# Field-pair products on one core: the order of a store's 128 rows inside its block of the output

## The chip, the cores and the metric

The kernel runs on one core of a Trainium2 chip. The metric is the device time of one execution in microseconds (us), less is better. Before the change it is 1285.48 us, the median of three runs.

## What is computed

The input is `x` with 4096 records of 32 fields of 64 numbers, and a 64 x 64 matrix `W`. Every field is multiplied by `W`, and for each of the 496 pairs of fields i < j the untouched field i is multiplied, number by number, with the transformed field j:

```python
vid = jnp.einsum('bfd,de->bfe', x, W)
idx_i, idx_j = jnp.triu_indices(32, k=1)
return x[:, idx_i, :] * vid[:, idx_j, :]        # 4096 x 496 x 64, float32
```

The output is 4096 x 496 x 64 x 4 bytes, 520 MB, against 33.6 MB of input. The order in which the kernel leaves the output in DRAM is its own choice: the host puts the numbers into the reference's order afterwards, and the time does not hold that step.

## The kernel before, in words

**Layout.** The 128 partitions of the on-chip memory are 2 halves of the batch times 64 numbers of a field. A "unit" is 128 records, 512 bytes in a partition. The 4096 records make 16 tiles of 2 x 128 records; a tile is 32 units of `x`, one for each field. The one large buffer `mem` (line 183) has 445 units in each partition, for the loaded `x` and the finished products together. PSUM holds `vid`, the 32 transformed fields of one tile.

**Work.** For each tile (loop at line 276) TensorE makes `vid` in two halves of 16 fields (lines 321 to 335), and VectorE forms the 496 products of the tile, one `tensor_tensor` for each run of pairs with one pattern (line 304). Over 16 tiles that is 7936 units of output in each partition. They are cut into 74 pieces, the `SLOTS` (line 28): each entry has the count n of units (48 to 128), the place in `mem` where they are put, and some seams at which a product is cut. 26 of the 74 slots have 128 units.

**Stores.** When the last product of a slot is made, `store` (line 261) sends it out as one DMA: 128 partitions with n units each. A partition's n units lie side by side in `mem` and in DRAM, so each partition is one row of n x 512 bytes, up to 65,536. The blocks of the slots lie one behind the other in the output (`BLOCKS`, line 62). Line 265 lays the rows in a block: row p, that is partition p, lies at place p of the block. After each of the two load groups one store is cut into a leading part of `LEAD` = 28 units and the rest (lines 267 to 270), so there are 76 stores.

**Order.** SP's queue (the issuing engine SyncE) carries the loads and the stores of slots 0 to 45, ScalarE's (ACT) those of slots 46 to 73 (`SECOND`, line 43). The input comes in two groups: tile 0 in two transfers and tiles 1 to 7 in three, at the start (lines 221 to 257); tiles 8 to 15 in three more in the middle (line 278). A store waits for VectorE's products (the semaphore `made`), and VectorE waits, before it writes units of `mem`, until the store that reads them has landed (`after`, line 204). The program sets these waits from the units that the transfers touch; the transfer and the waits are issued in `transfer` (line 197, the DMA itself line 199). There are 8 loads and 76 stores, 84 DMAs.

Of the kernel before, what the change touches and what calls it, by code (L numbers as in the profile page):

```python
# [10 lines left out]
P = 128  # L11

C = 128
# [30 lines left out]


LEAD = 28


PAD = 24
# [6 lines left out]
def row(n):  # L56

    return n
# [3 lines left out]
BLOCKS = [0, *accumulate(P * row(n) for n, *_ in SLOTS)]  # L62
# [112 lines left out]
def pairwise_bilinear_kernel(nc, x0, x, out):  # L175
# [8 lines left out]
    mem = ctx.enter_context(nc.sbuf_tensor([P, UNITS, C], F32))  # L184
# [3 lines left out]
    made = nc.alloc_semaphore("made")  # L188
# [8 lines left out]
    def transfer(out_, in_, units, reads, needs, queue=sp):  # L197
        sem = nc.alloc_semaphore(f"moved{len(moved)}")
        queue.issue(lambda: queue.engine.dma_start(out=out_, in_=in_), needs).then_inc(sem, 16)
        queue.note(sem, 16)  # L200
        moved.append((units, reads, sem))
        return sem
# [58 lines left out]
    def store(slot, last):  # L261
        nonlocal hold
        begin, end = STARTS[slot : slot + 2]
        home = SLOTS[slot][1]
        rows = out[BLOCKS[slot] : BLOCKS[slot + 1], :].rearrange("(p u) c -> p u c", p=P)
        parts = [(0, end - begin, (made, last), act if slot >= SECOND else sp)]
        if hold:
            early, late = ((sem, 16) for sem in hold[-2:])
            parts = [(0, LEAD, early, sp), (LEAD, end - begin, late, parts[0][3])]
            hold = []  # L270
        for lo, hi, need, queue in parts:
            units = (home + lo, home + hi)
            transfer(rows[:, lo:hi, :], mem[:, units[0] : units[1], :], units, True, [(made, last), need], queue)


    for t in range(NT):
        if t in begins[1:]:
            hold = load(begins.index(t))
            for late in held:
                store(*late)  # L280
            held = []
        xs = (place_of(t, F), place_of(t, F) + F)
        blocks = list(products(by_block(), t * NP))
        for k, (at, n, nest, i, j) in enumerate(blocks):
            slot = bisect_right(STARTS, at) - 1
            begin, end = STARTS[slot], STARTS[slot + 1]
            home = SLOTS[slot][1]
            units = (home + at - begin, home + at - begin + n)
# [21 lines left out]
            if at == end:  # L310
                late = (slot, counts[made])
                group = sum(behind <= slot for behind in STRETCHES)
                if t < begins[group]:
                    held.append(late)
                else:
                    store(*late)
# [65 lines left out]
```

## Time and profile before

| what | value |
|---|---|
| time, median of 3 runs | 1285.48 us (1285.39 to 1286.25) |
| time of the profiled execution | 1285.43 us |
| its span, first to last instruction | 1284.1 us |
| VectorE (DVE) busy | 1080.0 us, 84% of the span |
| TensorE (PE) busy | 181.8 us, 14% |
| read from HBM, written to HBM | 33.59 MB, 520.09 MB |

"Busy" is the time in which an engine runs an instruction; the profile gives its share of the span. The DMA share is the mean over the core's 16 DMA engines. A packet is one contiguous piece that a DMA engine moves, and the page counts them for each queue: q1 is SP's, q10 is ACT's. Times within the execution are counted from the start of the span. The chain of waits follows the last work back, each step to what released it.

### The profile page before, as it was taken

To read this page: it belongs to the slowest core of one execution; us is meant where nothing else is said; L and a number is where in the kernel's file an instruction comes from. 1 tells how busy PE (TensorE), PEld (TensorE's weight loads), DVE (VectorE), ACT (ScalarE), POOL (GpSimd) and SP (SyncE) were. 2 spreads that over 40 slices of the span, in tenths; PEclk is the share of its full clock that TensorE was granted. 3 is DMA by queue.
4 is the path that set the end of the run, shared out by engine and by line. 5 is a ranking of instruction groups with operands and counts; after the bars stand their busy time and mean duration, and the time that the engine had idled before them with its cause. 6 is when DMAs were issued, how large, how long until landed. Compare 5 with 4: busy or idle time off the path is not lost. (4 is left out here: it accounts for less than half of the span.)

```text
span 1284.1 us, 1255 instructions
## 1 busy us (share of the span) xinstructions
PE 181.8 (14%) x256; PEld 70.9 (6%) x256; DVE 1080.0 (84%) x273; POOL 0.2 (0%) x4
## 2 busy tenths in 40 slices
PE   2011120302111030300020112203020020201100
PEld 1000000100000010100010000001010010000000
DVE  6679979988897989998028989989998899899980
POOL 0000000000000000000000000000000000000000
PEclk8555565755666565655565655556565565756655
DMA  9999999999999999999999999999999999999999
GB/s 407 443 424 426 445 421 433 449 425 425 435 447 425 425 437 436 434 425 451 414 433 416 435 432 434 438 438 421 439 443 418 438 436 438 425 425 445 433 428 408
DMA packets 12098, 553.70 MB, mean 431 GB/s; under 512 B 1344, under 2 KB 1344, under 8 KB 1344
## 3 DMA queue, kind: packets, MB, share of 16 engines
q1 hardware_dynamic: 8064, 340.30, 61.5%
q10 hardware_dynamic: 4032, 213.39, 38.4%
q14 instruction: 2, 0.02, 0.0%
HBM read 33.59 MB, written 520.09 MB: 431 GB/s over the span
## 5 line engine op out<-in xcount | busy, mean ns | idle before, releaser
L304 DVE TENSOR_TENSOR mem<-mem,vid 128x1024 f32<-128x1024 f32 (+11 forms) x270 | 1079.5, 4067 | 162.2 <-DMA out_dram<-mem 112.9
L324 PE MATMUL vid<-mem,w 128*128 x256 | 181.8, 876 | 1014.3 <-PEq L322 1014.3
L324 PEld LDWEIGHTS vid<-mem,w 128*128 128x128 f32 x256 | 70.9, 291 | 1124.4 <-issue 1124.4
L233 DVE COPY w<-mem 64x64 f32<-64x64 f32 x2 | 0.4, 189 | 5.1 <-DMA mem<-in_r_x_dram 5.0
L230 DVE MEMSET w<- 128x128 f32 x1 | 0.2, 165 | 0.8 <-PEq L349 0.8
L349 POOL MEMSET const-bfloat16-1.0<- 128x1 bf16 x1 | 0.1, 101 | 0.0
L349 POOL MEMSET const-uint8-127<- 128x1 uint8 x1 | 0.1, 101 | 0.0
L349 POOL MEMSET const-float32-0.0<- 128x1 f32 x1 | 0.1, 98 | 0.2 <-issue 0.2
L349 POOL MEMSET const-float32-1.0<- 128x1 f32 x1 | 0.1, 98 | 0.0
## 6 DMA issues: line engine op xcount, KB each, us to landing
out_dram<-mem ACTq DMA_DIRECT2D x9, 7680.0 KB, 23.5
out_dram<-mem SPq DMA_DIRECT2D x3, 7680.0 KB, 23.2
out_dram<-mem ACTq DMA_DIRECT2D x3, 7168.0 KB, 21.6
out_dram<-mem SPq DMA_DIRECT2D x5, 4096.0 KB, 17.5
out_dram<-mem SPq DMA_DIRECT2D x3, 6656.0 KB, 20.8
out_dram<-mem SPq DMA_DIRECT2D x3, 5632.0 KB, 18.6
out_dram<-mem SPq DMA_DIRECT2D x2, 7168.0 KB, 22.6
out_dram<-mem SPq DMA_DIRECT2D x2, 6144.0 KB, 19.7
```

Of the source, the lines that this page charges most:

```text
L230: work(lambda: nc.vector.memset(w2[:, :], 0.0), [], [], made)
L233: lambda: nc.vector.tensor_copy(w2[half, half], mem[half, place + F, :D]),
L304: lambda: nc.vector.tensor_tensor(o, left, right, ALU.mult),
L324: last = nc.tensor.matmul(vid[:, b : b + BANK, :], lhsT=w2[:, :], rhs=xt(b), start=True, stop=True)
L349: nc = _bacc.Bacc("TRN2", target_bir_lowering=False, num_devices=1, dynamic_dma_scratch_size=512)
```

## The change

Only the order of the 128 rows inside a store's block changes. Write the partition as 8e + k, with e from 0 to 15 and k from 0 to 7. Before, row 8e + k lies at place 8e + k of the block; after, at place 16k + e. Rows that were 8 places apart, 8e and 8(e + 1), become neighbours, and neighbours 8e + k and 8e + k + 1 come to lie 16 places apart. The rows themselves, their lengths, the blocks, the number of DMAs, their queues, the loads, all waits and the leading parts of 28 units stay.

In the program the DRAM side of a store becomes a pattern with three counts, 16 by 8 by the row, where it was 128 by the row; the side of `mem` stays 128 by the row. The host's unpacking follows.

```diff
+RUN = 8
...
-        rows = out[BLOCKS[slot] : BLOCKS[slot + 1], :].rearrange("(p u) c -> p u c", p=P)
+        rows = out[BLOCKS[slot] : BLOCKS[slot + 1], :].rearrange("(k e u) c -> e k u c", k=RUN, e=P // RUN)
...
-            transfer(rows[:, lo:hi, :], mem[:, units[0] : units[1], :], units, True, [(made, last), need], queue)
+            transfer(rows[:, :, lo:hi, :], mem[:, units[0] : units[1], :], units, True, [(made, last), need], queue)
...
-    got = [got[a:b].reshape(P, -1, C)[:, :n] for a, b, (n, *_) in zip(BLOCKS, BLOCKS[1:], SLOTS)]
+    got = [
+        got[a:b].reshape(RUN, P // RUN, n, C).transpose(1, 0, 2, 3).reshape(P, n, C)
+        for a, b, (n, *_) in zip(BLOCKS, BLOCKS[1:], SLOTS)
+    ]
```

## The prediction, made before the changed kernel ran

> **What bounds the kernel now.** I read the page's first three parts, then the stages, then the waits. The page first:
>
> ```profile
> PE 181.8 (14%) x256; PEld 70.9 (6%) x256; DVE 1080.0 (84%) x273; POOL 0.2 (0%) x4
> ...
> DMA  9999999999999999999999999999999999999999
> ...
> DMA packets 12098, 553.70 MB, mean 431 GB/s; under 512 B 1344, under 2 KB 1344, under 8 KB 1344
> ...
> q1 hardware_dynamic: 8064, 340.30, 61.5%
> q10 hardware_dynamic: 4032, 213.39, 38.4%
> ...
> HBM read 33.59 MB, written 520.09 MB: 431 GB/s over the span
> ```
>
> VectorE is busy for 84% of the span, but the DMA engines for 61.5 + 38.4 = 99.9% of it, in every one of the 40 slices. So the transfers are the bound and VectorE has about 200 us to spare. The packet count says how a DMA is cut: 84 DMAs in 12,096 packets are 144 each, that is 128 rows and 16 tiny ones (84 x 16 = 1344, the packets under 512 B). A row is one packet, and each of 16 engines carries 8 rows of a DMA and one tiny packet. From q10: 28 DMAs have 28 x 128 = 3584 rows, in 0.384 x 1284.1 x 16 = 7889 us of engine time, 2.20 us a row; 213.39 MB in that time are 27.0 GB/s for one engine.
>
> Now by stage: loads alone, stores from SP, stores from ACT, and the end.
>
> ```profile
> 4.00:30.00 26.00, 8.60 (x16) 3.59 (x16) 18.09 (x8) 0.00 (x0) 0.81 1.03 443
> 100.00:600.00 500.00, 76.92 (x104) 29.62 (x104) 466.17 (x111) 0.00 (x0) 0.57 1.00 433
> ...
> 900.00:1270.00 370.00, 44.71 (x64) 17.52 (x64) 324.04 (x72) 0.00 (x0) 0.57 1.00 434
> ```
>
> The last two columns are the DMA share and GB/s. (Packets are counted whole in the window in which they start, so a short window can show more than 1.) Loads run at 443 / 1.03 = 430 GB/s, stores at 433 and 434, from either queue. Reading HBM and writing it give the same rate within 1%. A limit in HBM would hardly give the same number both ways; a limit that each DMA engine meets on its own way to the on-chip memory would, and 27 GB/s for each of 16 is what the rows show. So **the engines go at their own ceiling, one way each, and nothing is left over**: a faster HBM gives nothing, and whatever makes an engine slower is paid in full.
>
> The waits say the same from the other side:
>
> ```profile
> DVE mem L304 <- DMA out_dram<-mem: 112.9, 35, 18.5
> DVE mem L304 <- PE vid L324: 49.0, 2, 43.1
> ```
>
> VectorE waits 112.9 us in 35 places for stores to give room in `mem` free. Stores wait for VectorE only in form: the DMA engines have no gap.
>
> One thing more is needed, how evenly the 16 engines go. The end shows it:
>
> ```profile
> 1278.00:1281.00 3.00, 0.00 (x0) 0.00 (x0) 0.00 (x0) 0.00 (x0) 0.50 1.14 492
> 1281.00:1281.50 0.50, 0.00 (x0) 0.00 (x0) 0.00 (x0) 0.00 (x0) 0.50 1.99 860
> 1281.50:1282.00 0.50, 0.00 (x0) 0.00 (x0) 0.00 (x0) 0.00 (x0) 0.50 0.28 123
> 1282.00:1282.40 0.40, 0.00 (x0) 0.00 (x0) 0.00 (x0) 0.00 (x0) 0.50 0.00 0
> ```
>
> In 1281.0 to 1281.5 rows with 1.99 x 0.5 x 16 = 15.9 us of engine time start, seven of the 16 last rows; one more starts in the next half microsecond (0.28 x 0.5 x 16 = 2.2 us), and then none. So after 1280 us the 16 engines begin their last row within about a microsecond of one another: they go in step. I take 0.65 us as the offset between two of them, an estimate from these two windows.
>
> **The change part by part.** Nothing is computed differently; the 8 loads, VectorE's 273 instructions and TensorE's matmuls stay, and they stand beside the transfers (200 us of VectorE's span is free). Only line 265's pattern differs, in 76 stores, 520.09 of 553.70 MB. At 431 GB/s that is 520.09 / 0.431 = 1206.7 us of the span.
>
> Where the rows land in HBM: the same bytes, in the same rows of up to 64 KiB, in the same blocks. Since HBM does not set the rate, I price this at nothing. The bounds: a gain would be at most 431 against the best long stage's 434 GB/s, 1284.1 - 553.70 / 0.434 = 8.3 us, of which some 4 us are the start without data and the landing of the last store; a loss would have to make HBM slower than 431 GB/s for writes to one stretch of 16 rows, 1 MiB, for which no row speaks.
>
> Issuing: a pattern with one more count can take the queue longer to issue. A store is issued well before the engines get to it:
>
> ```profile
> out_dram<-mem ACTq DMA_DIRECT2D x9, 7680.0 KB, 23.5
> ```
>
> 7680 KB take 7.86 MB / 0.434 = 18.1 us, so 5.4 of the 23.5 us lie before and after the transfer, beside the previous store's data. A microsecond more of issuing is covered by these. Without that cover it would be 76 us for each microsecond.
>
> **Which engine gets which rows** is the part that can cost. Before, both sides of a store have 128 as outermost count; now the DRAM side has 16 and the side of `mem` 128. If the work is dealt by the outermost counts, the only equal deal among 16 engines gives engine e the DRAM index e, that is partitions 8e to 8e + 7 in this order; the names in the diff fit that. How 128 rows against 128 were dealt, the trace does not record. If it was the same deal, nothing changes. If it was one under which each engine has a way of its own into the on-chip memory, the new deal can put two engines on one way at a time. Between these two the rows speak for the second in one respect: 16 engines in step, all at 27 GB/s all the time, need 16 ways that never meet, and a deal made by counting off eight neighbours need not have that. The upper bound is that each way serves two engines and carries no more than the 27 GB/s that one draws today: every row then takes twice as long. Lower bound nothing, or the gain above.
>
> [...]
>
> The sum for two engines on one way: each of a store's halves of four rows takes 4 x 2.20 = 8.8 us alone, and twice that when both engines want the same way; an offset between the two is subtracted, since while one is ahead it has the next way to itself. Fully in step: 1284.1 + 1206.7 = 2490.8 us. With an offset of 0.65 us, twice in each of 76 stores, 2 x 76 x 0.65 = 98.8 us less: 2392 us of span, and with the 1.3 us around the span (1285.43 against 1284.1) 2393. The profiled execution is 0.05 us from the median, so this stands against the median as well. VectorE (1080 us) and the loads stay hidden or as they are. I choose the upper part of the bounds because the engines' step of under a microsecond against 8.8 us is the nearest row there is to how they would meet. Own range of this case: 2150 (offsets of 2.2 us, one row) to 2492.
>
> **The rivals.**
>
> *Two engines on one way, but they drift apart.* [...] For it: only a little unfairness is needed. Against: the end windows show engines that do not drift when alone. Rows broken into smaller packets would come out in this stretch too; the 144 packets for a DMA are what would change. 1310 to 2150 us.
>
> *Not slower: the deal keeps every engine's way its own, and writes become neighbours in HBM.* [...] It decides if no two engines meet; the price is then bounded by the engines' own ceiling: from 1281 us (half of the 8.3 us gained) to 1288, most likely 1285. For it: the rows show no loss in HBM to be had either way, and every engine still has 8 rows of the same length. Against: only the dealing. [...]
>
> *The change does not do what it says.* If the engines take rows in another order than eight neighbours, the rows written at one time are no neighbours; bytes and rows are the same, and it is 1285 us again, in the same case.
>
> **How the numbers follow.** Forecast (both engines of a pair in step): 0.50. Drift or a partial meeting: 0.22. Not met: 0.28, of it 0.05 faster by over 0.2% (2.6 us, which needs most of what the ceiling leaves), 0.17 within 0.2%, and 0.06 slower by some microseconds for issuing. 0.2% is about what a measurement of this kernel can tell from no change. Slower: 0.50 + 0.22 + 0.06 = 0.78. The range must reach over the case without a meeting, since leaving it out would leave out more than 2 in 10: from 1283 to 2492 us. The likeliest case alone is 2150 to 2492, and its value 2393.
>
> **What would show it.** If right: loads at 4 to 30 us still near 430 GB/s; stores near 220 to 240 GB/s with the DMA engines still about 100% busy; 12,098 packets as before; VectorE's wait for stores up from 112.9 to over 1000 us; a 7680 KB store landing over 38 us after its issue. Drift would show as a rate that climbs through the slices. The forecast is wrong if stores keep 430 GB/s, which would mean that no two engines meet, or if the packet count rises, which would mean another cause.

## The result and the profile after

The changed kernel takes 2121.85 us (median of six runs, 2105.23 to 2144.86) against 1285.95 us (six runs, too): 1.6485 times as long, 95% interval 1.6434 to 1.6537. The profiled execution is the longest of the six, 2144.86 us, a slow one that the ratio leaves out, so its rows are about 1% above the median.

The page of the changed kernel, the lines that answer to those shown of before:

```profile
PE 185.5 (9%) x256; PEld 72.5 (3%) x256; DVE 1082.7 (51%) x273; POOL 0.2 (0%) x4
...
DMA  9999999999999999999969999998999999999997
GB/s 377 260 329 260 241 257 260 258 224 231 261 261 267 258 243 245 254 264 270 299 225 265 280 277 244 240 254 257 239 252 235 251 266 267 223 241 245 268 273 213
DMA packets 12098, 553.70 MB, mean 258 GB/s; under 512 B 1344, under 2 KB 1344, under 8 KB 1344
...
q1 hardware_dynamic: 8064, 340.30, 58.2%
q10 hardware_dynamic: 4032, 213.39, 38.7%
```

The same packets carry the same bytes, and the DMA engines are busy for 58.2 + 38.7 = 96.9% of a span that is 1.67 times as long. So they are not short of work: each row takes them longer. VectorE's own 1082.7 us are nearly as before (1080.0); it has become the engine that waits. As these lines show (96.9% at 258 GB/s, where it was 99.9% at 431), a busy share close to 100% says only that a packet is under way, not that it moves at full rate; only beside GB/s can the two be told apart.

By stage, loads alone and two stretches of stores (columns as before, the last two the DMA share and GB/s):

```profile
4.00:30.00 26.00, 9.60 (x16) 3.90 (x16) 17.00 (x8) 0.00 (x0) 0.79 1.03 446
100.00:600.00 500.00, 53.96 (x72) 20.96 (x72) 286.54 (x79) 0.00 (x0) 0.54 0.98 258
1200.00:2000.00 800.00, 75.66 (x104) 29.46 (x104) 432.64 (x113) 0.00 (x0) 0.54 0.98 251
```

The loads, which the change leaves alone, run at 446 GB/s with share 1.03, as before (443); the stores fell from 433 to 258 and 251 GB/s. The waits, and the time of one store:

```profile
DVE mem L307 <- DMA out_dram<-mem: 916.2, 65, 45.5
```

```profile
out_dram<-mem ACTq DMA_DIRECT2D x9, 7680.0 KB, 60.1
```

VectorE waits 916.2 us for stores, 112.9 before. A store of 7680 KB on ACT's queue lands 60.1 us after its issue (median of nine), 23.5 before, though at 258 GB/s its bytes need 30.5 us. Part of the rest is that the last of a store's 16 parts now lands long after the first, 17.6 us in the median of all DMAs, as the landing times further down show.

The trace also has each packet's duration. For the 1536 rows of 61,440 bytes (stores of 120 units), worked out from the trace:

```
rows of 61,440 B, us:      under 2.5   2.5-3   3-3.5   3.5-4   4-4.5   4.5-5   over 5   median
before                          1536       0       0       0       0       0        0     2.27
changed kernel                   387      60      90      91     186     646       76     4.42
```

Before, every row takes 2.27 us. After, rows fall into two heaps: a quarter at the old time and nearly half (722 of 1536 over 4.5 us) at about twice that. This is not a general slowing of 1.65 times; it is one of about two, for part of the rows.

### The profile page after: what moved, and what is told of

Same layout as the page of the kernel before. It is cut to its first block, busy times and chain, and to the rows that moved or that the text cites. A ratio compares the mean times of both kernels' runs of the same rounds, so it can differ in the third digit from the quotient of the medians.

```text
span 2143.5 us, 1255 instructions
## 1 busy us (share of the span) xinstructions
PE 185.5 (9%) x256; PEld 72.5 (3%) x256; DVE 1082.7 (51%) x273; POOL 0.2 (0%) x4
## 2 busy tenths in 40 slices
DMA packets 12098, 553.70 MB, mean 258 GB/s; under 512 B 1344, under 2 KB 1344, under 8 KB 1344
## 3 DMA queue, kind: packets, MB, share of 16 engines
q1 hardware_dynamic: 8064, 340.30, 58.2%
q10 hardware_dynamic: 4032, 213.39, 38.7%
## 5 line engine op out<-in xcount | busy, mean ns | idle before, releaser
L307 DVE TENSOR_TENSOR mem<-mem,vid 128x1024 f32<-128x1024 f32 (+11 forms) x270 | 1082.1, 4069 | 981.7 <-DMA out_dram<-mem 916.2
## 6 DMA issues: line engine op xcount, KB each, us to landing
out_dram<-mem ACTq DMA_DIRECT2D x9, 7680.0 KB, 60.1
```

Source lines behind the costliest of these rows:

```text
L307: lambda: nc.vector.tensor_tensor(o, left, right, ALU.mult),
```

## The experiments

Three theories stood against each other. The deal, here, is which DMA engine gets which rows. **A**, the new deal lets two engines meet on one way into the on-chip memory; **B**, the new places in HBM are slow to write; **C**, a pattern with one more count is slow to carry out. The first four kernels ran on one chip, beside a kernel before of 1285.69 us.

### The same deal, the old order in HBM

```diff
-BLOCKS = [0, *accumulate(P * row(n) for n, *_ in SLOTS)]
+BLOCKS = [0, *accumulate(P * row(n) + P // RUN for n, *_ in SLOTS)]
...
-rows = out[...].rearrange("(k e u) c -> e k u c", k=RUN, e=P // RUN)
+rows = out[...].rearrange("(e r) c -> e r c", e=P // RUN)
+rows = rows[:, : RUN * (end - begin), :].rearrange("e (k u) c -> e k u c", k=RUN)
```

> The DRAM pattern keeps the counts 16 by 8 of the changed kernel, but the rows lie in the order of the kernel before (row 8e + k behind row 8e + k - 1), with one spare unit of 512 bytes behind every eight rows so that the pattern cannot be folded to 128. Theory A (the 16 engines get eight neighbouring partitions each, and two of them meet on one way into the on-chip memory): as slow as the changed kernel, 2050 to 2200 us. Theory B (the new order of rows in HBM is slow to write): about 1286 us, since the order is the old one. Theory C (a pattern with one more count is slow to carry out, whatever the counts): 2050 to 2200 us.

Measured: 2137.38 us (2117.71 to 2149.16), ratio 1.6575 (1.651 to 1.6639). The rows lie as before but for 512 bytes behind every eight rows, and all of the loss is there; the stores run at the changed kernel's rate. B falls.

```profile
100.00:600.00 500.00, 52.91 (x73) 20.80 (x74) 292.77 (x82) 0.00 (x0) 0.55 0.99 264
```

### Reordered in HBM, with 32 as outermost count

```diff
-RUN = 8
+RUN = 4
```

> RUN is 4: row 4b + k lies at place 32k + b, a DRAM pattern with 32 by 4 by the row. [...] Theory A: the meeting is gone, 1283 to 1290 us. Theory B: rows written at one time lie next to each other as in the changed kernel, about 2100 us. Theory C: about 2100 us.

Measured: 1286.27 us, ratio 1.0003 (0.9994 to 1.0012). Its stages:

```profile
4.00:30.00 26.00, 9.09 (x16) 3.75 (x16) 17.79 (x8) 0.00 (x0) 0.83 1.03 444
100.00:600.00 500.00, 73.95 (x104) 28.73 (x104) 465.97 (x111) 0.00 (x0) 0.58 1.00 433
```

Stores run at 433 GB/s, the rate before, with a pattern of three counts and with rows that lie 32 places from their partition's neighbour. C falls, and B a second time: neither the extra count nor the places cost anything, nor do they bring anything. What is left is the outermost count: with 128 and 32 the stores run at 433 GB/s, with 16 at 258. It is not that fewer engines share the work, since the DMA share, a mean over all 16, is still 0.98 in the changed kernel. That the meeting is gone with 32 was the author's estimate: the trace does not record which engine carries a row, and shows the rate alone.

### Half the partitions at a time

```diff
-transfer(rows[:, lo:hi, :], mem[:, units[0] : units[1], :], ...)
+halves = (slice(0, D), slice(D, P))          # D = 64
+transfer(tuple(rows[h, lo:hi, :] for h in halves),
+         tuple(mem[h, units[0] : units[1], :] for h in halves), ...)   # two DMAs, one semaphore
```

> The kernel before, places and plain pattern unchanged, but each store is two DMAs, one of partitions 0 to 63 and one of 64 to 127, on the same queue. Theory A: each of the two reaches only half of the ways, so two engines meet unless one of them is already in the other half: slower by as much as the changed kernel or more, 1950 to 2490 us. Theories B and C: nothing they speak of has changed; 1286 us, at most 1300 with the added issues.

Measured: 2136.18 us in one run. Plain pattern, old places, and nearly the time of the changed kernel (its runs: 2105 to 2145). The stores run at its rate, too:

```profile
100.00:600.00 500.00, 55.38 (x72) 21.33 (x72) 287.26 (x79) 0.00 (x0) 0.54 0.98 261
```

B and C have nothing to say to this: the loss is there without any reordering. This kernel also has twice as many store DMAs, so that the partitions are the cause is shown only by the next one, which keeps that number.

### The same half twice

```diff
-         tuple(mem[h, units[0] : units[1], :] for h in halves), ...)
+         tuple(mem[:D, units[0] : units[1], :] for h in halves), ...)
```

> As the store in two halves, but both DMAs of a store read partitions 0 to 63, so that half of the products is left out of the output and the other half written twice; bytes, rows and places are the same. No engine can find a free way in the other half by being ahead. Theory A: every row takes twice as long whatever the offsets, 78 us for loads and 2 x 1207 us for stores, 2450 to 2520 us, and more than the store in two halves. Theories B and C: 1286 to 1300 us.

The kernel leaves the products of partitions 64 to 127 out of its output. Measured: 2622.70 us in one run, 486 us more than with both halves, with the same DMAs, bytes and places. Only the partitions that the second DMA reads differ: 0 to 63 in place of 64 to 127. So the source in the on-chip memory sets the rate: 207 GB/s here, 261 with both halves. The time is over the 2450 to 2520 expected, and the stages show why:

```profile
4.00:30.00 26.00, 9.87 (x16) 4.04 (x16) 17.01 (x8) 0.00 (x0) 0.79 1.03 445
100.00:600.00 500.00, 40.67 (x56) 15.91 (x56) 222.70 (x63) 0.00 (x0) 0.54 1.00 207
```

Stores run at 207 GB/s, 0.48 of 433, and of its 1536 rows of 61,440 bytes 1535 take between 4.5 and 5 us, median 4.79. That is the second heap of the changed kernel, by itself. If every row here meets another, a meeting makes a row 4.79 / 2.27 = 2.11 times as long, not twice. That 64 partitions reach half of the ways was the author's estimate; how many ways there are, and which partitions share one, these runs do not show.

### Every store begun in step

```diff
+prior = [(stored, 16)] if stored else []          # the store before must have landed
-transfer(..., [(made, last), need], queue)
+stored = transfer(..., [(made, last), need, *prior], queue)
```

The kernel before with this edit, as the measure for the next:

> The kernel before, where each store also waits until the store before it has landed, so that the 16 engines begin every store in step and no store follows another without a gap. The gaps are the same in this kernel and in its partner with the changed layout: an estimate from 5.4 us between transfer time and landing, 2 to 5 us for each of 76 stores, 1430 to 1670 us.

Measured: 1394.55 us in one run. The gaps are (1393.3 - 1284.1) / 76 = 1.4 us of span a store, less than the 2 to 5 expected, and the time is under the 1430 to 1670.

> The changed kernel with the same wait. If the changed kernel came out below 2393 us because its engines drift apart during the run (the offset being subtracted), starting every store in step takes that away: this kernel is slower than its partner by 1100 to 1207 us. If a meeting of two engines simply costs less than double, and drift has no part, the difference stays near that of the two kernels themselves, 2122 - 1286 = 836 us. If rows are slow for their places in HBM, also about 836 us.

Measured: 2706.62 us in one run, 1312 us over its partner; 836 us were the difference without the wait. The stores from 100 to 600 us, first the partner, then the changed layout:

```profile
100.00:600.00 500.00, 79.64 (x104) 30.69 (x104) 428.61 (x109) 0.00 (x0) 0.56 0.92 397
```

```profile
100.00:600.00 500.00, 41.63 (x51) 16.11 (x52) 219.24 (x62) 0.00 (x0) 0.52 0.92 196
```

The same DMA share of 0.92, and 196 against 397 GB/s: when all engines begin a store together, nearly every row takes about twice as long. Of the 1536 rows of 61,440 bytes 1323 take over 4.5 us, where it was 722 in the changed kernel, and none under 3. So what keeps the changed kernel at 2122 us, below the 2622.70 of the low half, is that its engines run out of step. The 1312 us are more than the 1207 upper limit expected, by 1.09, which the 2.11 of the low half covers.

### The same deal for loads

```diff
+wide = (x.shape[1] - 1) // 8
...
+x = x[:, : 8 * wide, :].rearrange("e (k u) c -> e k u c", k=8)     # x padded by one unit behind 8 rows
...
-x[:, at : at + hi - lo, :]
+x[:, :, at : at + hi - lo, :]
```

> The kernel before with its stores as they were; only the six large loads (tiles 1 to 15, 31.5 of 33.6 MB) get the counts 16 by 8, by one spare unit behind every eight rows of the input in DRAM. It moves the question to the other direction. If the meeting is at the on-chip memory (theory A), writing into it suffers too: 31.5 MB take 73 us at 430 GB/s and up to 2.1 times that, 81 us more, less where the engines are out of step: 1320 to 1367 us, and the start, up to the first store's end, is visibly slower. If it belongs to writing HBM, or only to reading the on-chip memory, nothing changes: 1284 to 1290 us.

Measured: 1359.22 us in one run, against 1286.77 beside it, within the 1320 to 1367 expected. The stages of this kernel:

```profile
4.00:30.00 26.00, 9.16 (x16) 3.75 (x16) 17.65 (x8) 0.00 (x0) 0.83 1.09 258
30.00:60.00 30.00, 0.00 (x0) 0.00 (x0) 10.73 (x4) 0.00 (x0) 0.50 0.97 202
100.00:600.00 500.00, 81.71 (x112) 31.82 (x112) 460.21 (x116) 0.00 (x0) 0.58 1.00 434
```

The loads now run at 258 and 202 GB/s where the kernel before has 443 and, in the second stretch, in which its stores have begun, 440:

```profile
30.00:60.00 30.00, 0.00 (x0) 0.00 (x0) 17.43 (x6) 0.00 (x0) 0.50 1.02 440
```

The untouched stores run at 434. In this kernel's first 60 us HBM is only read (its first store is issued at 73.5 us). So the loss comes in both directions with the same deal, and is no property of HBM writes. That it arises at the on-chip memory is shown for stores by the low half; for loads it is carried over.

## Why the prediction came out as it did

**The bound: right.** The DMA engines were the bound, 99.9% busy before and 96.9% after. What slowed the rows was paid nearly in full: VectorE's work is unchanged, and its wait rose by 916.2 - 112.9 = 803 us of the 859 by which the span grew.

**Places in HBM at nothing, issuing at nothing: right.** The 32 by 4 kernel shows both at once, 1.0003. Counted from partition to partition, the new order puts rows of 64 KiB 16 places or 1 MiB apart, where they lay side by side; with 32 by 4 they are 32 places or 2 MiB apart, and nothing is lost. The rivals that end without a loss needed a deal that costs nothing; that deal exists, with 32 as outermost count (1286.27 us), but it is not the one of this change. "Does not do what it says" is out too: reordering with 32 by 4 does move the rows and is free.

**The deal: right in what it costs a row.** With an outermost 16, many rows take about twice as long (722 of 1536 over 4.5 us, against 2.27), as nearly all do in the low-half kernel (1535 of 1536), where only the partitions that are read were changed; its rate is 0.48 of the rate before. That two engines share a way, and that an engine gets eight neighbours, were the author's estimate. The trace does not record which engine carries a row, so neither this deal nor any pair of engines was seen by itself.

**The sum: two sizes off, in opposite directions.** The price of everything meeting was put at 1206.7 us; the low half alone gives 2621.4 - 1284.1 = 1337 us, since a row there takes 2.11 and not 2 times as long. The offset's term was put at 98.8 us, from 0.65 us twice in each of 76 stores. No run shows that term, a store in two halves of four rows for each engine with 8.8 us and an offset in each; what the runs show in its place is rows of 2.27 and of about 4.8 us and, from the low-half kernel down to the changed one's median less the 1.3 us around the span, a difference of 2621.4 - 2120.6 = 501 us, that is 6.6 us a store. Together 131 more and 402 less: 2393 became 2122. The time is just below the forecast's own stretch, which ends at 2150 (its sum with an offset of one row, 2.2 us, gives 2158), and in that of the rival in which engines drift apart. Both were at work: 722 of the 1536 rows take over 4.5 us, and the parts of a DMA come to land a median of 17.6 us apart.

The step that failed is that the 16 engines "go in step", read at the end of the kernel before and carried over to the changed one. It holds where no row is slowed: the last of a DMA's 16 parts lands a median of 0.69 us after the first in the kernel before and 0.72 with 32 by 4. The end of the changed kernel:

```profile
2095.00:2105.00 10.00, 0.00 (x0) 0.00 (x0) 0.00 (x0) 0.00 (x0) 0.50 1.04 287
2105.00:2115.00 10.00, 0.00 (x0) 0.00 (x0) 0.00 (x0) 0.00 (x0) 0.50 0.93 287
2115.00:2125.00 10.00, 0.00 (x0) 0.00 (x0) 0.00 (x0) 0.00 (x0) 0.50 0.70 215
2125.00:2135.00 10.00, 0.00 (x0) 0.00 (x0) 0.00 (x0) 0.00 (x0) 0.50 0.61 160
2135.00:2143.50 8.50, 0.00 (x0) 0.00 (x0) 0.00 (x0) 0.00 (x0) 0.50 0.10 43
```

The share falls from 1.04 to 0.10 over some 40 us: the engines run out of rows far apart, where they began their last rows within about a microsecond before. In the trace's landing times, the last part comes 0.7 to 0.8 us after the first for each of the five loads at the start; then this grows over the first stores, and the median over all 84 DMAs is 17.6 us. Worked out from the trace:

```
last landing minus first, us, in order of landing (five loads, then the first seven stores)
before    0.7  0.7  0.7  0.7  0.7  0.6  0.6  0.6  0.5  0.5  0.5  0.5
changed   0.8  0.8  0.8  0.8  0.7  2.2  4.4  7.9 10.3 13.0 16.8 13.1
```

**The rival of drift: half right.** Engines do fall out of step, but the rate does not climb through the slices, which was the sign of drift: 260 GB/s in the second slice and 251 from 1200 to 2000 us. The rate fell by 433 / 258 = 1.68, and the 1536 rows take 3.85 us on average, 1.69 times the 2.27. If a row that meets another takes 2.11 times as long, 0.69 / 1.11 = 0.62 of them meet, an estimate from these times. Why drift that goes on does not bring that down is not shown: the trace does not name the engine of a packet, and no run held an offset fixed. Why one engine gets ahead of another at all is open as well. It hardly happens where both DMAs of a store read the same 64 partitions. With the first 16 landings of a store counted for its first DMA, these lie a median of about 3 us apart in the low-half kernel and about 14 in the kernel with two halves.

**The signs named beforehand.** Loads near 430: yes. Packets 12,098: yes. DMA engines about 100% busy: 96.9%. Stores at 220 to 240 GB/s: 251 to 258, for the offset. VectorE's wait over 1000 us: 916.2, for the same reason. A 7680 KB store over 38 us: 60.1, since its last part counts.

## What to carry to other kernels

A DMA's outermost count was not only bookkeeping here: on 128 partitions, 128 or 32 on the DRAM side kept the full 433 GB/s, 16 took 1.65 times as long, and 64 partitions at a time 1.66 times (one run). If a reordered DRAM pattern is wanted, try outer groups of four partitions, as 32 by 4 does here (433 GB/s), and test it with one look at GB/s beside the DMA share. When the DMA share stays near 100% while GB/s falls, as here with 96.9% and 258 GB/s, look for what makes each row take longer, not for missing work; and do not carry over an offset measured where no row is slowed: 0.69 us between first and last landing before became 17.6 in the changed kernel.

## What the runs showed that was not expected

With stores that read 64 partitions throughout, the 16 engines move less than half of what they move with 128: a row takes 4.79 us instead of 2.27, and the stage has 207 instead of 433 GB/s, 0.96 of half. If two engines share a way there, they move less together than one alone. Landing before the next store is issued costs only 1.4 us a store (1394.55 against 1285.8 us, 109 us in all) when VectorE has time to spare, while in the changed layout this same wait puts the engines in step and adds 585 us (2706.62 against 2121.85), 476 more.
